# Six expert pairs of eight by seven block products, with projection weights fetched from DRAM, in a fused attention and mixture-of-experts kernel

## The chip, the cores and the metric

The kernel runs on one core of a Trainium2 chip. The metric is the device time of one execution in microseconds. A core has five engines with instruction queues of their own: TensorE (PE, its weight loads shown as PEld), VectorE (DVE), ScalarE (ACT), GpSimd (POOL) and SyncE (SP), which here issues every transfer (DMA). Work on different engines is ordered by semaphores alone.

## The reference

A layer of linear attention and a dense mixture of experts, each followed by a layer norm, on 8 sequences of 1024 tokens with 256 features, in float32:

```python
qkv = x @ Wqkv + bqkv;  q, k, v = split(qkv, 3)
q = q - mean(q); k = k - mean(k)
q2 = q*q; q2 = l2norm(q2 / (sum(q2) + 1e-7), over features)
k2 = k*k; k2 = l2norm(k2 / (sum(k2) + 1e-7), over tokens)
kv = einsum('bnc,bnd->bcd', k2, v)
t2 = einsum('bnc,bcd->bnd', q2, kv) / sqrt(1024)
x  = layernorm(x + (v + t2) @ Wln + bln)
sel    = sigmoid(einsum('bsd,ed->bse', x, expert_sel))      # 16 experts
scores = relu(einsum('bsd,edh->bseh', x, keys))             # 128 hidden each
x  = layernorm(x + einsum('bseh,ehv,bse->bsv', scores, values, sel))
```

Every expert is computed for every token, so the experts' two products are most of the arithmetic.

## The kernel before

**Tiles.** The 8192 tokens are cut into 16 chunks of 512 (`c`, two to a sequence). Every float32 operand of a product is kept as a high and a low part (`h` and `l`), and a product is made of three matmuls: high by high, high by low, low by high (`passes3`). For a chunk the kernel projects k (`u_k`, PSUM tile `kp`) and q (`u_q`, `qp`), forms the sums over tokens (`ap`, `asb`), and for each sequence the matrix `mh`/`ml` (`u_m`, `mc` and `pm`). `u_y` makes the normalised-to-be rows `ych`/`ycl` (`yp`), and the gates, which go to DRAM and come back spread over all partitions, a row per expert (`gates_of`, tile `selb`, L1014). `u_weights` loads and splits the experts' keys and values once, in four groups of four experts.

**Experts.** In a chunk the 16 experts are taken in 8 pairs (`u_pair`). A plain expert (`plain1`) makes `h` = keys by `y`: six matmuls of 512 columns. Then `gated` (L1039 to L1041) multiplies by the gate on DVE, casts to the high part `sh` on ACT and subtracts for the low part `sl` on DVE. `ffn2` (L1121) multiplies by the values into two banks `w0`, `w1`, which gather all 16 experts: six matmuls an expert.

**Seven products.** A pair's `h` is a product of a 2 by 2 block matrix of keys (two experts by two halves of the features) with a 2 by 2 block matrix of `y` (two halves of the features by two halves of the tokens). `fast1` does it with seven block products in place of eight, in the manner of Strassen and Winograd: 7 x 3 = 21 matmuls of 256 columns (L1074) into two banks `hx` and `hy`, in place of 12 of 512. It needs sums of key blocks (`u_sums`, tiles `ksh`/`ksl`; made once for a pair, on POOL and ACT, from `ksr`) and combinations of `y` blocks (`u_t`; once a chunk: `y` and `tu` on POOL, `th` on ACT, `tl` on DVE or POOL). Between its matmuls four copies of half a bank are made by ACT (L1083, L1084, L1087, L1090), and one addition by DVE (L1093). Pairs 4 to 7 (`FAST_PAIRS`) go this way, from chunk 1 (`FAST_FROM`).

**Order.** The order is planned before the program is written. Each piece of work is a task with its engine or engines, an assumed cost, a key (its due time, in units of one expert) and the buffers that it reads and writes. `Work.order` plays the tasks through in assumed time: at each moment an idle engine takes the ready task with the least key, no further ahead of the oldest open task than `WINDOW`, for which its buffers are free. The constants `AT_...` shift the keys of the stages. The instructions are then issued engine by engine in the order of their planned starts. Each engine, and SP's queue of transfers, runs strictly in that order. The part ahead of the first experts (`goals`, `tail`) is ordered by `sharpen`, which repeats a list schedule forwards and backwards 24 times and keeps the shortest; where PE has nothing to do there, it is given warming matmuls (`warm`).

**Buffers.** SBUF tiles come from rings by tag (`SB_SLOTS`): six `t4` buffers of 4 KB per partition, four `t2` of 2 KB, three `ld2` for loads, two `selb`, and so on. PSUM has four banks `h` (for `h`, `hx`, `hy`), two `att` for the attention, and `w0`, `w1`. The projections' weights `wkh`, `wkl`, `wqh`, `wql`, `wvlh`, `wvll`, `wyh`, `wyl` and the key sums are constants, in SBUF from beginning to end.

Of the kernel before, what the change touches and what calls it, by code (L numbers as in the profile page):

```python
# [15 lines left out]
P = 128  # L16
# [11 lines left out]
WINDOW = 10.47  # L28
# [3 lines left out]
FAST_AT = 0.39  # L32
AT_Y, AT_YEND, AT_X, AT_N, AT_K, AT_Q, AT_M, AT_END = 2.04, 4.17, 0.95, 0.19, 5.21, 12, 16.28, -0.91
AT_Q1, AT_K2, AT_W1, AT_W2, AT_W3, AT_SUMS, AT_SEL = -30, -19.9, -10.93, -7.7, 8.8, 8.58, 7
EAGER = 3.73
BOOST = 2.0
RESERVE = {"att": 1}
FAST_PAIRS = range(4, 8)
# [3 lines left out]
    "ld2": 3, "xh": 2, "xl": 2, "s4": 4, "ych": 2, "ycl": 2, "sh": 2, "sl": 2, "selb": 2, "gt": 2, "t4": 6, "t2": 4,  # L42
    "v1": 2, "g0": 4, "g1": 4, "g2": 4, "g3": 4, "acc": 1, "asb": 1, "mh": 1, "ml": 1, "tiny": 14,
# [58 lines left out]
class Work:  # L102
# [13 lines left out]
    def add(self, eng, cost, key, fn, r=(), w=(), port=False, after=()):  # L116
# [6 lines left out]
        for many, writes in ((r, False), (w, True)):  # L123
            for x in many:
                b, part = x if isinstance(x, tuple) else (x, None)
                for other, opart, owrites in b.accesses:
                    if (writes or owrites) and meet(part, opart) and other is not t:
                        t.deps.add(other)
                b.accesses.append((t, part, writes))
                t.bufs[b] = None  # L130
        for d in t.deps:
            d.outs.append(t)
# [50 lines left out]
    def sharpen(self, rounds=24):  # L183
# [7 lines left out]
        rank, best = {t: t.tail for t in part}, None  # L191
        for _ in range(rounds):
            start = self.pack(part, deps, rank, {})
            span = max(start[t] + x for t, x in self.goals.items())
            if best is None or span < best[0]:
                best = span, start
            back = self.pack(part, outs, start, release)
            rank = {t: back[t] + min(t.cost.values()) for t in part}
# [3 lines left out]
    def order(self):  # L202
# [24 lines left out]
        while left:  # L227
# [7 lines left out]
            while moved:  # L235
# [5 lines left out]
                for e in free:  # L241
# [3 lines left out]
                    for entry in ready[e]:  # L245
# [7 lines left out]
                        if e == "G" and first and t.tail is None and t.port[e]:  # L253
                            continue
# [68 lines left out]
def attn_ffn_kernel(ctx, tc, x, xT, wqT, wk, wvT, wlnT, bcols, brows, selT, keys, values, outT):  # L323
# [55 lines left out]
    def high(key, h, b, n, r, w, free=True):  # L379

        if free:
            add("VS", {"V": c_dve(n, fast=True), "S": c_act(n, plain=True)}, key,
                {"V": lambda: V.tensor_copy(h(), b()), "S": lambda: S.copy(h(), b())}, r=r, w=w, port={"V": True, "S": False})
        else:
            add("S", c_act(n, plain=True), key, lambda: S.copy(h(), b()), r=r, w=w)

    def apply(key, out, a, b, op, n, r, w, engines="VG"):
# [3 lines left out]
        if len(engines) == 1:  # L391
            add(engines, cost[engines], key, fns[engines], r=r, w=w, port=True)
        else:
            add(engines, cost, key, fns, r=r, w=w, port={"V": True, "G": True})
# [10 lines left out]
    def cbuf(name, shape, dtype=F32):  # L405
# [4 lines left out]
    wkh, wkl, wqh, wql, wvlh, wvll, wyh, wyl = (  # L410
        cbuf(n, [P, 2, D], FR) for n in ("wkh", "wkl", "wqh", "wql", "wvlh", "wvll", "wyh", "wyl")
    )
# [47 lines left out]
    def centered_rows(key, b, h, l):  # L460
# [8 lines left out]
        for k in range(2):  # L469
            add("VS", {"V": c_dve(D, fast=True, ptr=True), "S": c_act(D)}, key, {  # L470
                "V": lambda k=k: V.tensor_scalar(h[:, k], b[:, k], m[:, k : k + 1], None, ALU.add),
                "S": lambda k=k: S.activation(h[:, k], b[:, k], AF.Identity, bias=m[:, k : k + 1]),
            }, r=[b, m], w=[(h, k)], port={"V": True, "S": False})
            add("V", c_dve(D, ptr=True), key, lambda k=k: V.scalar_tensor_tensor(
                l[:, k], b[:, k], m[:, k : k + 1], f(h[:, k]), ALU.add, ALU.subtract), r=[b, m, (h, k)], w=[(l, k)], port=True)
# [15 lines left out]
    def high_low(key, t, h, l):  # L491
        add("S", c_act(CH, plain=True), key, lambda: S.copy(h.ap, halves(t.ap)), r=[t], w=[h])
        add("V", c_dve(CH), key, lambda: V.tensor_tensor(l.ap, halves(t.ap), f(h.ap), ALU.subtract), r=[t, h], w=[l])
# [23 lines left out]
    def split(c, key, name, src, h, l, width):  # L517
# [3 lines left out]
        for i in range(n):  # L521
# [4 lines left out]
            high(key + 1.2, lambda s=s: h[:, s], lambda b=b: b.ap, 2 * CH // n, [b], [(h, part)], c < 2)  # L526
# [16 lines left out]
    def project(c, g, t, wh, wl, bias=None):  # L543
        for j in range(2):
            tk = slice((2 * g + j) * P, (2 * g + j + 1) * P)
            terms = []
            for k in range(2):
                terms += passes3(xh[c][:, k, tk], xl[c][:, k, tk], wh[:, k, :], wl[:, k, :])
# [19 lines left out]
    def u_k(c, key):  # L568
        b = c // PER_B
        even = c % PER_B == 0  # L570
# [5 lines left out]
        for g in range(2):  # L576
            tt = slice(2 * g, 2 * g + 2)
            t = psum(f"kp{c}_{g}", "h" if c == 0 else "att")
            if c < 2:
                add("T", c_mm(D, 14), key + g, lambda g=g, t=t: project(c, g, t, wkh, wkl, 1),  # L580
                    r=x_parts(c, g) + [wkh, wkl, rows, bhl], w=[t])
                squares(key + g + 0.7, q, g, s, t)
                continue
            add("T", c_mm(D, 12), key + g, lambda g=g, t=t: project(c, g, t, wkh, wkl), r=x_parts(c, g) + [wkh, wkl], w=[t])
# [5 lines left out]
        for g in range(2):  # L590
# [3 lines left out]
            high(key + 3.5 + g * 0.3, lambda tt=tt: h[:, tt, :], lambda tt=tt: q[:, tt, :], CH, [(q, tt)], [(h, g)], c < 2)  # L594
# [16 lines left out]
        if even:  # L611
            asb[b], acc[b] = sbuf("asb", [P, CH], f"asb{b}"), sbuf("acc", [P, 2, D], f"acc{b}")
# [24 lines left out]
    def u_m(b, key):  # L637
        cs, kn, ky, ka = (tiny(f"{n}{b}") for n in ("cs", "kn", "ky", "ka"))
        ah, al = sbuf("t2", [P, 2, D], f"ah{b}", FR), sbuf("t2", [P, 2, D], f"al{b}", FR)
        mh[b], ml[b] = sbuf("mh", [P, 2, D], f"mh{b}", FR), sbuf("ml", [P, 2, D], f"ml{b}", FR)  # L640
# [31 lines left out]
        def mmm(ct):  # L672
            cols = slice(ct * P, (ct + 1) * P)
            terms = []
            for k in range(2):
                terms += passes3(ah[:, k, cols], al[:, k, cols], wvlh[:, k, :], wvll[:, k, :])
            mm_group(pm[:, ct * D : (ct + 1) * D], terms)

        add("T", c_mm(D, 12), key + 1, lambda: (mmm(0), mmm(1)), r=[ah, al, wvlh, wvll], w=[pm])
# [24 lines left out]
    def u_q(c, key):  # L704
        q = sbuf("t4", [P, 4, D], f"q{c}")
        s, n2, y, a = (tiny(f"{n}{c}") for n in ("qs", "qn", "qy", "qa"))
        q2h[c], q2l[c] = (sbuf("s4", [P, 2, CH], f"{t}{c}", FR) for t in ("q2h", "q2l"))
        for g in range(2):
            tt = slice(2 * g, 2 * g + 2)
            t = psum(f"qp{c}_{g}", "h" if c == 0 else "att")  # L710
            if c < 2:
                add("T", c_mm(D, 14), key + g, lambda g=g, t=t: project(c, g, t, wqh, wql, 0),
                    r=x_parts(c, g) + [wqh, wql, rows, bhl], w=[t])
                squares(key + g + 0.7, q, g, s, t)
                continue
            add("T", c_mm(D, 12), key + g, lambda g=g, t=t: project(c, g, t, wqh, wql), r=x_parts(c, g) + [wqh, wql], w=[t])
# [132 lines left out]
    def u_y(c, key):  # L849
        b = c // PER_B  # L850
        ych[c], ycl[c] = yh, yl = [sbuf(t, [P, 2, CH], f"{t}{c}", FR) for t in ("ych", "ycl")]
        sq = sbuf("t4", [P, 2, CH], f"ysq{c}")

        def ymx(t, jt):
            cols = slice(jt * P, (jt + 1) * P)
            terms = []
            for k in range(2):
                terms += passes3(wyh[:, k, cols], wyl[:, k, cols], xh[c][:, k, :], xl[c][:, k, :])
# [9 lines left out]
        for jt in range(2):  # L868
            t = psum(f"yp{c}_{jt}", "h" if c == 0 else "att")
            k0 = key + jt  # L870
            add("T", c_mm(CH, 6), k0, lambda t=t, jt=jt: ymx(t, jt), r=[xh[c], xl[c], wyh, wyl] + ([] if c == 0 else [mh[b], ml[b], q2h[c], q2l[c]]), w=[t])
# [96 lines left out]
    sums_h, sums_l, th, tl = {}, {}, {}, {}  # L968

    def u_sums(p, key):  # L970

        g, e = p // 2, p % 2 * 2
        h, l = sums_h[p], sums_l[p] = [cbuf(f"ks{n}{p}", [P, 3, P], FR) for n in "hl"]
# [8 lines left out]
        add("S", c_act(3 * P, plain=True), key + 1, lambda: S.copy(h.ap, u[:, three]), r=[u], w=[h])  # L982
        add("S", c_act(P, plain=True), key + 1.1, lambda: S.copy(keyh[g][:, e + 1, 0], u[:, 3]), r=[u], w=[(keyh[g], last)])
        apply(key + 1.5, lambda: l.ap, lambda: u[:, three], lambda: f(h.ap), ALU.subtract, 3 * P, [u, h], [l], "G")
# [3 lines left out]
    def u_t(c, key):  # L988
# [3 lines left out]
        for k in range(2):  # L992
            apply(key, lambda k=k: y[:, k], lambda k=k: f(yh[:, k]), lambda k=k: f(yl[:, k]), ALU.add, CH, [yh, yl], [(y, k)], "G")
# [23 lines left out]
    def u_pair(c, p):  # L1017
# [6 lines left out]
        if c >= FAST_FROM and p in FAST_PAIRS:  # L1024
# [34 lines left out]
    def fast1(c, p, key, sel, a, b):  # L1059
# [6 lines left out]
        sum_ = lambda i: (sums_h[p][:, i], sums_l[p][:, i])  # L1066
# [10 lines left out]
        old, new = [(keyh[g], pair), (keyl[g], pair)], [sums_h[p], sums_l[p]]  # L1077
# [312 lines left out]
```

## Time and profile before

| | us |
|---|---|
| median of 3 runs (1020.59 to 1023.46) | 1022.59 |
| the profiled execution | 1020.05 |
| its span, first to last instruction | 1018.3 |
| PE, DVE, ACT, POOL busy | 1008.1, 784.8, 667.1, 470.5 |
| first `w` matmul (start of the experts' second product) | 63.96 |

The page gives for each engine the busy time, its share of the span and the number of instructions. The chain is the work that ended last, followed backwards. A row of the timeline has its start, its duration, engine, line, operation and `out<-in` by the program's names; in brackets the engine's idle time before it and what ended that. A row of the chain in order of time has start, duration, engine and tile. A row of the waits has who waited for whom, the total in us, how often, and the longest. A row of the stretches has the busy time of each engine in it, with the granted clock of PE, the share of the DMA engines and GB/s at its end. A row of the transfers has its number, size and median time from issue to landing.

### The profile page before, as it was taken

What the parts mean: (1) busy time and instruction counts of PE and PEld (TensorE: products, weight loads), DVE (VectorE), ACT (ScalarE), POOL (GpSimd) and SP (SyncE); (2) the same over time, 40 slices, a digit from 0 to 9 for tenths busy, and PEclk for the clock granted to TensorE, in tenths of its full rate; (3) what the DMA queues carried; (4) which work ended last, traced back from release to release, by engine and by line L of the source; (5) the groups of instructions that cost most, each with busy time, mean ns of one, the idle gap of its engine ahead of it and who ended that gap; (6) DMA issues with size and microseconds to landing.
All of it is one profiled execution on the core that took longest, in us unless ns stands there. A gap on an engine that the chain in (4) does not pass through costs nothing.

```text
span 1018.3 us, 16317 instructions
## 1 busy us (share of the span) xinstructions
PE 1008.1 (99%) x5757; PEld 874.3 (86%) x5757; DVE 784.8 (77%) x1363; ACT 667.1 (66%) x1497; POOL 470.5 (46%) x424
## 2 busy tenths in 40 slices
PE   9999999999999999999999999999999999999996
PEld 9978879888898988889888888988889888888885
DVE  7889888687776887768787687867878687686775
ACT  7767566675676757766676676757666675665543
POOL 1001585546564464655536574454654536233430
PEclk9999999999999999999999999999999999999999
DMA  6144323233232323323223231323323222223131
GB/s 202 44 135 125 116 94 125 93 90 101 82 121 68 115 94 104 93 89 103 93 89 108 87 115 63 115 94 103 105 71 109 93 85 83 83 85 104 64 125 42
DMA packets 65298, 99.52 MB, mean 98 GB/s; under 512 B 6336, under 2 KB 24896, under 8 KB 65216
## 3 DMA queue, kind: packets, MB, share of 16 engines
q1 hardware_dynamic: 65216, 98.48, 30.1%
q8 instruction: 45, 0.74, 0.3%
q14 instruction: 37, 0.30, 0.1%
HBM read 89.54 MB, written 8.91 MB: 97 GB/s over the span
## 4 chain that ended last, share of the span: by engine, by line
PE 93%; DVE 3%; POOL 2%; ACT 1%; DMA 1%; issue 1%; POOLq 0%; DVEq 0%; ACTq 0%; SPq 0%
PE w L1121 32%; PE h L358 17%; PE hx L1074 11%; PE yp L358 8%; PE qp L358 4%; PE hy L1074 4%; PE kp L358 4%; PE ap L358 4%; PE warm L435 1%; PE qt L755 1%; PE sp L358 1%; PE pm L358 1%; DMA ksr<-keys 1%; PE mc L358 1%; DVE sl L1041 0%
## 5 line engine op out<-in xcount | busy, mean ns | idle before, releaser
L1121 PE MATMUL w<-sh,valh 128*128 128x512 f32 x504 | 158.4, 395 | 0.0
L1121 PE MATMUL w<-sh,vall 128*128 128x512 f32 x504 | 158.0, 394 | 0.0
L1121 PE MATMUL w<-sl,valh 128*128 128x512 f32 x504 | 157.7, 394 | 0.0
L1039 DVE SCALAR_TENSOR_TENSOR h<-h,selb 128x512 f32<-128x512 f32 x136 | 93.9, 692 | 31.0 <-PE h L358 27.8
L1121 PEld LDWEIGHTS w<-sh,vall 128*128 128x128 f32 x504 | 95.0, 188 | 22.1
L1121 PEld LDWEIGHTS w<-sl,valh 128*128 128x128 f32 x504 | 94.6, 188 | 22.4
L1040 ACT CAST sh<-h 128x512 fp32r<-128x512 f32 x136 | 73.6, 589 | 59.6 <-PE w L1121 55.5
L358 PE MATMUL h<-ych,keyh 128*128 128x512 f32 x272 | 109.7, 403 | 0.0
L358 PE MATMUL h<-ycl,keyh 128*128 128x512 f32 x272 | 107.5, 395 | 0.0
L358 PE MATMUL h<-ych,keyl 128*128 128x512 f32 x272 | 107.0, 393 | 0.0
L1041 DVE TENSOR_TENSOR sl<-h,sh 128x512 fp32r<-128x512 f32 x136 | 87.8, 683 | 23.1 <-ACT sh L1040 23.0
L1121 PEld LDWEIGHTS w<-sh,valh 128*128 128x128 f32 x504 | 86.2, 188 | 10.9
L389 POOL TENSOR_TENSOR k<-k,ks 128x512 f32<-128x512 f32 x25 | 30.9, 1257 | 101.9 <-DVE ks L566 101.9
L1093 DVE TENSOR_TENSOR hx<-hx,p 128x512 f32<-128x512 f32 x60 | 41.8, 696 | 29.8 <-ACT hy L1090 29.6
L1135 POOL TENSOR_TENSOR w<-w,ycl 128x512 f32<-128x512 f32 x30 | 38.2, 1296 | 55.5 <-DVE w L1132 55.5
L389 POOL TENSOR_TENSOR ysq<-ysq 128x512 f32<-128x512 f32 x15 | 20.1, 1338 | 91.1 <-ACT ysq L875 91.1
L358 PEld LDWEIGHTS h<-ych,keyl 128*128 128x128 f32 x272 | 51.1, 188 | 12.0
L358 PEld LDWEIGHTS h<-ycl,keyh 128*128 128x128 f32 x272 | 51.3, 189 | 10.5
L358 PEld LDWEIGHTS h<-ych,keyh 128*128 128x128 f32 x272 | 51.1, 188 | 10.7
L877 DVE SCALAR_TENSOR_TENSOR ycl<-yp,by,ych 128x512 fp32r<-128x512 f32 x32 | 24.0, 750 | 42.9 <-ACT ysq L875 42.9
L1090 ACT COPY hy<-hx 128x256 f32<-128x256 f32 x60 | 21.4, 357 | 46.9 <-PE hx L1074 45.4
L389 POOL TENSOR_TENSOR q<-q,qy 128x512 f32<-128x512 f32 x27 | 28.1, 1060 | 51.3 <-ACT sh L1040 43.7
(505 smaller groups left out, 3193.6 us busy)
## 6 DMA issues: line engine op xcount, KB each, us to landing
selb<-sel SPq DMA_DIRECT2D x253, 256.0 KB, 3.5
xf<-xT SPq DMA_DIRECT2D x30, 256.0 KB, 3.3
outT<-w SPq DMA_DIRECT2D x15, 512.0 KB, 3.0
nf<-x SPq DMA_DIRECT2D x28, 256.0 KB, 4.6
kst<-keys SPq DMA_DIRECT2D x6, 256.0 KB, 3.3
vst<-values SPq DMA_DIRECT2D x6, 256.0 KB, 3.7
nf<-x SPq DMA_DIRECT2D x2, 512.0 KB, 7.9
ksr<-keys SPq DMA_DIRECT2D x4, 256.0 KB, 3.5
```

The lines of the kernel that those rows point to most:

```text
L358: T.matmul(out, w, r, start=first and i == 0, stop=last and i == len(terms) - 1)
L389: fns = {e: (lambda e=e: ENG[e].tensor_tensor(out(), a(), b(), op)) for e in engines}
L435: T.matmul(warm[:, :P], ones.ap, ones.ap, start=True, stop=True)
L877: add("V", c_dve(CH, ptr=True), k0 + 0.9, lambda t=t, jt=jt: V.scalar_tensor_tensor(yl[:, jt, :], t.ap, by[:, jt : jt + 1], f(yh[:, jt, :] ...
L1039: add("V", c_dve(CH), key + 0.1, lambda: V.scalar_tensor_tensor(at(t.ap), at(h.ap), 0.0, out(sel), ALU.max, ALU.mult), r=[h] + reads(sel), ...
L1040: add("S", c_act(CH, plain=True), key + 0.1, lambda: S.copy(out(a), at(t.ap)), r=[t], w=reads(a))
L1041: add("V", c_dve(CH), key + 0.1, lambda: V.tensor_tensor(out(b), at(t.ap), f(out(a)), ALU.subtract), r=[t] + reads(a), w=reads(b))
L1074: T.matmul(out(), wi, ri, start=first and i == 0, stop=True, skip_group_check=True)
L1090: add("S", c_act(n, plain=True), key + 0.07, lambda: S.copy(y1(), x1()), r=[x], w=[y])
L1093: add("V", c_dve(CH), key + 0.09, lambda: V.tensor_tensor(halves_(x.ap), halves_(x.ap), p5.ap.to_broadcast([P, 2, n]), ALU.add), r=[x, p5] ...
L1121: T.matmul(wps[c][v].ap, w[:, e % 4, v * P : (v + 1) * P], r[:, i], start=e == 0 and j == 0, stop=e == NE - 1 and j == 2)
L1135: add("G", c_pool(CH), key + 0.5, lambda v=v: G.tensor_tensor(w[:, v, :], w[:, v, :], f(ycl[c][:, v, :]), ALU.add), r=[(w, v), ycl[c]], w= ...
```

## The change

It has three parts that hang together.

1. Pairs 2 to 7 go by seven products. Pairs 4 to 7 begin in chunk 1 as before, pairs 2 and 3 in chunk 2 (`FAST_LATER`).
2. To make room, the projections' weights are no longer constants. Each set of high and low parts is one tile of four blocks. It is made in a buffer that later serves something else (`FIRST_AT`), stored to DRAM (`keep`), used there for the first one to three times (`FIRST_USES`), and after that fetched for each use into one of two buffers `wt` (`weight`), 512 KB at a time, one fetch after another in the plan. The key sums of a group of two pairs share a tile `kk1` to `kk3`, which the first weights leave. `t4` has seven buffers, `t2` five; `acc`, `asb`, `mh` and `ml` share a ring `m2` of three.
3. A task can hold buffers that it does not touch (`hold`): the first task of `u_t` takes `y`, `tu`, `th` and `tl` together, and a cast takes the buffer of the low part with that of the high.

Also, `sharpen` goes on with 110 random trials after its 24 rounds, a rule with `GIVE` can keep an engine free for an opening task, and the constants of the order have new values.

```diff
-WINDOW = 10.47
+GIVE = 9.0
+WINDOW = 9.25
-FAST_AT = 0.39
+FAST_LATER = 2
+FIRST_AT = {"k": "kk1", "q": "kk2", "y": "kk3", "v": "t4"}
+FIRST_USES = {"k": 3, "q": 2, "y": 1, "v": 1}
+FETCH = 7.22
+AT_KEEP = -42.59
+FAST_AT = -0.74
-FAST_PAIRS = range(4, 8)
+FAST_PAIRS = range(2, 8)
...
-    "ld2": 3, ... "t4": 6, "t2": 4,
-    "v1": 2, ... "acc": 1, "asb": 1, "mh": 1, "ml": 1, "tiny": 14,
+    "ld2": 3, ... "t4": 7, "t2": 5,
+    "v1": 2, ... "m2": 3, "wt": 2, "kk0": 1, "kk1": 1, "kk2": 1, "kk3": 1, "tiny": 14,
...
+        for b in hold:
+            b.accesses.append((t, None, False))
+            t.bufs[b] = None
...
-    wkh, wkl, wqh, wql, wvlh, wvll, wyh, wyl = (
-        cbuf(n, [P, 2, D], FR) for n in ("wkh", "wkl", "wqh", "wql", "wvlh", "wvll", "wyh", "wyl")
-    )
+    first_w = {n: sbuf(t, [P, 4, D], f"w{n}", FR) for n, t in FIRST_AT.items()}
+    kept_w, fetched = {}, []
+
+    def keep(name, key):
+        w, d = first_w[name], work.buf("dram", [P, 4, D], F32, f"w{name}_kept")
+        add("D", 2.1, key, lambda: nc.sync.dma_start(out=d.ap, in_=f(w.ap)), r=[w], w=[d])
+        kept_w[name] = d
+
+    def weight(name, use, key):
+        if use < FIRST_USES[name]:
+            return first_w[name]
+        w, d = sbuf("wt", [P, 4, D], f"w{name}{use}", FR), kept_w[name]
+        fetched[:] = [add("D", 2.1, key - FETCH, lambda: nc.sync.dma_start(out=f(w.ap), in_=d.ap), r=[d], w=[w], after=fetched)]
+        return w
...
     def u_k(c, key):
         b = c // PER_B
+        wt = weight("k", c, key)
...
-    sums_h, sums_l, th, tl = {}, {}, {}, {}
+    sums, sums_, th, tl = {}, {}, {}, {}
+    since = lambda p: FAST_FROM if p >= 4 else FAST_LATER
...
-            apply(key, lambda k=k: y[:, k], ..., ALU.add, CH, [yh, yl], [(y, k)], "G")
+            apply(key, lambda k=k: y[:, k], ..., ALU.add, CH, [yh, yl], [(y, k)], "G", (u, th[c], tl[c]))
...
-        if c >= FAST_FROM and p in FAST_PAIRS:
+        if c >= since(p) and p in FAST_PAIRS:
             fast1(c, p, key, sel, a, b)
...
-        if c == FAST_FROM - 1:
-            for p in FAST_PAIRS:
+        for p in FAST_PAIRS:
+            if c == since(p) - 1:
                 u_sums(p, NE * c + 2 * p + AT_SUMS)
```

`u_q`, `u_y` and `u_m` call `weight` in the same way as `u_k`.

## The prediction

> **What bounds the kernel now.** I read the page first, for the share of each engine and the chain that ended last.
>
> ```profile
> span 1018.3 us, 16317 instructions
> PE 1008.1 (99%) x5757; PEld 874.3 (86%) x5757; DVE 784.8 (77%) x1363; ACT 667.1 (66%) x1497; POOL 470.5 (46%) x424
> ...
> q1 hardware_dynamic: 65216, 98.48, 30.1%
> ...
> PE 93%; DVE 3%; POOL 2%; ACT 1%; DMA 1%; issue 1%; POOLq 0%; DVEq 0%; ACTq 0%; SPq 0%
> ```
>
> TensorE is busy for 99% of the span and carries 93% of the chain. Since matmuls are pipelined, a busy PE may still hide gaps, so I next read the chain in order of time, which gives the pace at which matmuls follow one another.
>
> ```profile
> 171.42 1.42 PE hx L1074 x12
> ...
> 208.17 1.40 PE h L358 x6
> ```
>
> Six matmuls of 512 columns take 1.40 us, 233 ns each; twelve of 256 columns take 1.42 us, 118 ns each. Half the columns cost half the time, so TensorE streams columns without gaps in both forms. Two views say where it does not: the waits of the matmuls themselves (two, 2.0 us in the whole run) and the busy time by stretches.
>
> ```profile
> PE hx L1074 <- ACT p L1084: 0.9, 1, 0.9
> ...
> 0.00:70.00 70.00, 68.94 (x457) 62.45 (x458) 56.82 (x143) 51.08 (x128) 4.11 (x13) 0.98 0.40 124
> ...
> 557.00:618.00 61.00, 61.00 (x349) 52.89 (x349) 46.82 (x81) 40.69 (x92) 33.56 (x29) 1.00 0.30 96
> ...
> 984.00:1018.30 34.30, 26.02 (x170) 23.04 (x169) 22.64 (x40) 12.70 (x30) 0.00 (x0) 0.94 0.18 62
> ```
>
> From 70 to 1008 us TensorE is full (61.00 of 61.00) while VectorE has 47, ScalarE 41, GpSimd 34 of 61 us; the clock is 1.00. Only the start (to the first `w` matmul at 63.96 us) and the tail (about 10 us after 1008) are bound by something else. So in the long middle a microsecond less of matmul columns is a microsecond less of span, as long as the other queues keep up.
>
> **The change, part by part.**
>
> *Pairs by seven products.* The orders of the two programs, compared engine by engine, give PE 336 fewer `h` matmuls of 512 columns (816 to 480), and 588 more of 256 (`hx` 900 to 1320, `hy` 360 to 528). That is 28 pairs: pairs 2 and 3 in chunks 2 to 15. By the pace above: 336 x 1.40/6 = 78.4 us go, 588 x 1.42/12 = 69.6 us come, **-8.8 us**, all in the stretch where PE is full.
>
> Here a rule speaks against the change. Weight loads in this trace last 188 ns each (`PEld`, every shape), and the Trainium skill, "Perfetto Trace Analysis", section "Identifying the Most-Contended Engine", says that TensorE's headroom is to be judged by the share of LDWEIGHTS time and not of matmul time. Each converted pair raises the loads from 12 to 21. If the 188 ns were what TensorE is spaced by, a pair would go from 2.79 us (12 x 233 ns, columns) to 21 x 0.188 = 3.95 us, and 28 pairs would add 32 us. But the row above shows twelve 256-column matmuls, each with a load of its own, in 1.42 us: loads overlap one another and start every 118 ns. The sum is -8.8 by the row, about +32 by the rule; the row decides. PEld's share should rise (252 more loads) with no cost.
>
> *Hand-overs inside a pair.* A seven-product pair has four ScalarE copies between its matmuls. The trace gives their latency:
>
> ```profile
> 993.96 0.28 PE L1074 MATMUL hx<-th,ksl 128*128 128x256 f32 x1
> ...
> 994.33 0.36 ACT L1087 COPY hx<-hx 128x256 f32<-128x256 f32 x1 [0.27 <-PE hx L1074]
> ```
>
> From the start of the last matmul to the end of the copy it is 0.73 us, of which that matmul's own slot is 0.12, so with a little for the semaphore the next matmul needs about 0.65 us of other PE work in between. By the new order, priced at the paces above, each such gap holds 0.93 us or more, except two: in pair 2 of chunks 2 to 14 three `hy` and four transposes follow the `hx` (0.35 + 0.44 = 0.79 us), and in chunk 15 only the three `hy` (0.35). In the ScalarE queue the cast of the preceding expert stands ahead of that copy. Bounds: nothing; or a whole cast late (0.59 us) 13 times plus 0.3, 8 us. In the old trace weight loads of `hx` and `hy` waited 5.8 + 2.1 us for ScalarE over 60 pairs, nearly all under a running matmul, so I take **+1.0**, range 0 to 8.
>
> *Left and right operands earlier.* The combinations `t` of a chunk (u_t: POOL `tu`, ACT `th`, then `tl`) are now needed at pair 2 instead of pair 4. In chunk 5 the old trace has the last `tl` at 367.5 and the first `hx` at 393.4 us: 26 us spare. By the PE order, from the end of the k projection that precedes it on POOL to the first `hx` there were 50 us of matmuls, now 34, so some 10 us stay spare. In chunk 2 POOL also makes the key sums of two more pairs (u_sums: 5 x 0.46 + 1.02 = 3.3 us each). It can lose up to 3 us once; a gain is possible too, since a 1.05 us stop before the first `hx` of chunk 1 may go. I take 0. Taking four `t4` buffers at once can only delay `y`, and comes out of the same spare time.
>
> *VectorE, ScalarE, GpSimd.* Per converted pair one more DVE addition (696 ns) and four copies (371 + 365 + 361 + 357 ns). DVE +19.5 us, plus 11 `tl` moved to it from POOL (each 0.7 to 1.6 us by the rows, 8 to 18): 812 to 822 of about 1010, 81%. ACT +40.7: 708, 70%. POOL falls by 11 x 1.32 = 14.5 and gains 6.6. All stay below PE's 99%: 0 us; if DVE's cover were gone, a late gate would cost what it lacks.
>
> *Weights from DRAM.* SP issues 49 fetches and 4 stores of 512 KB and two `ksr` more (374 to 429 transfers): 28.3 MB on 98.5, so the queue's share goes from 30% to about 39%. The nearest row is the 512 KB output:
>
> ```profile
> outT<-w SPq DMA_DIRECT2D x15, 512.0 KB, 3.0
> ```
>
> A fetch waits until PE has finished with the use before last (two `wt` buffers). By the PE order at least 19.6 us of matmuls lie between that release and the next use: 3.0 us is covered sixfold, 0 us. Behind a fetch on SP's queue stand the gate rows (`selb`). Those are not short either:
>
> ```profile
>   PE h L358: 27.8, 28
>   DMA selb<-sel: 2.9, 3
> ```
>
> VectorE sat idle for gates in three places, 2.9 us in all. A 3.0 us transfer ahead of them should fit. If it doesn't, see the first rival.
>
> *The start.* The search for the opening order has more tries, and group 2's weights now come before group 1's, but the same matmuls stand ahead of the first `w`; two more warming matmuls are issued, in a place where PE waits for gates (0 to 0.9 us; six of them took 2.63). The four stores leave SP in the time in which it stood 29 us at one transfer (14.41 to 43.43). Bounds -1 to +2; I take **+0.3**.
>
> *The tail* is the same code: 0.
>
> **Sum:** -8.8 + 1.0 + 0.3 = -7.5 us. The profiled execution took 1020.05 us, its span 1018.3; the forecast for it is 1012.6. The median of the three runs, 1022.59, lies 2.5 above it, and so does the forecast: **1015.1 us**. A measurement of this kernel can tell about 0.3%, 3.1 us, from no change.
>
> **The rivals.**
> *Gates behind fetches (slower).* SP's queue is in order, and it already spends much of its time waiting for gate buffers (320.0 us at `selb` for VectorE's `h`). If a fetch waits longer than the gate behind it can bear, VectorE's gating stops, the `h` banks aren't freed, and PE stops. It turns the change into a loss once the 49 fetches cost more than 0.15 us each (7.5 us); half of a 3.0 us transfer lost at every third is already 24 us. For it: the queue's waits. Against: the spare time of gates (2.9 us of waits in 253) and the 19.6 us lead. I put it at about 1028 us (0.26 each).
> *Hand-overs eat it (no change).* Pair 2's copy comes 0.5 us late in 13 chunks, and `tl`, twice on DVE while POOL holds the shared memory port (1.63 us at the median in the old trace against 0.67 at the least), is late before the first `hx` in the odd chunks. That costs 6.5 more: 1021.5 us.
> *The rate of 256 columns is not half.* If loads bound somewhere, up to +32 us; the row excludes it for these very tiles.
> That it does not do what it says is excluded by the order.
>
> **How the numbers follow.** Forecast 0.80 (1010.5 to 1019.5, by the bounds of the hand-overs and the start), hand-overs eat it 0.12, gates 0.08. The range 1011.5 to 1021.5 takes in the second case's middle and leaves out the gates and the best end of the first. Faster by over 0.3%: 0.80; within: 0.12; slower: 0.08.
>
> **What would show it.** Right: PE still at 61.00 of 61 in the middle, `h` x480 and `hx` at 118 ns, DVE near 81%, q1 near 39%, the first `w` near 64 us. Wrong: waits of VectorE for `selb` of tens of us (first rival), or of PE or PEld for `hx`/`tl` copies, repeated at pair 2 of each chunk (second).

## The result, and the profile after

The changed kernel is slower: 1034.51 us at the median of four runs (1034.01 to 1036.34), against 1022.91 for the kernel before beside it. The ratio is 1.0121, with an interval of 1.0101 to 1.0141. The forecast was 1015.1, and its range ended at 1021.5. The profiled execution took 1036.34 us, its span is 1034.6, which is 16.3 more than before.

These are the page's lines that answer to those of before: span, busy time of each engine, the transfer queue, the chain that ended last.

```profile
span 1034.6 us, 17084 instructions
...
PE 1011.6 (98%) x6013; PEld 885.1 (86%) x6013; DVE 824.0 (80%) x1399; ACT 704.0 (68%) x1615; POOL 468.2 (45%) x426
...
q1 hardware_dynamic: 73904, 126.79, 38.3%
...
PE 59%; DVE 13%; ACT 9%; issue 3%; POOL 1%; DMA 1%; ACTq 0%; DVEq 0%; POOLq 0%
```

The numbers that the forecast gave for these rows are nearly right: DVE 824.0 (forecast 812 to 822), ACT 704.0 (708), the queue 38% (39). What is new stands in the last line: DVE carries 13% of the chain and ACT 9%, where they carried 3 and 1. (PE's 59% can't be set beside the 93% of before: this chain could be followed back to 143.7 us only, so its shares add up to 86%.) Where PE loses time, a busy share doesn't tell, as the middle stretch shows (columns: PE, PEld, DVE, ACT, POOL busy, granted clock, DMA share, GB/s):

```profile
557.00:618.00 61.00, 60.70 (x370) 53.80 (x369) 47.37 (x78) 44.38 (x103) 27.72 (x23) 1.00 0.38 123
```

PE still shows 60.70 of 61, although it loses time, because the end of a matmul is modelled and covers short gaps. So I counted stalls from the starts: where the next matmul begins later than the pace of its form (232 ns for 512 columns, 118 for 256, some 110 for less), the excess is a stall; those of over 40 ns between 66 and 1000 us are added up. Before they come to 6.0 us, after to 30.9. The pace itself is unchanged. With the 8.8 us of fewer columns the sum closes: -8.8 + 24.9 = +16.1, measured +16.3. The start is no part of it (first `w` matmul at 64.1 us, before 63.96).

This sum is that of two single executions. The profiled one of the change was the slowest of its four and that of before lay 2.9 us under its median, so that 16.3 us stands here for the 11.6 between the medians. And for 3.4 us, from 507.8, the granted clock of the change was at half (third number from the right; 0.64 is the mean of a wider stretch), which makes some 1.5 us of the 30.9:

```profile
506.50:511.00 4.50, 3.96 (x15) 3.38 (x16) 3.42 (x7) 2.14 (x5) 0.17 (x1) 0.64 0.29 90
```

Of the 30.9 us, 24.0 belong to the odd chunks: 11.3 at `hx` of pair 2, 4.0 at `hy` of pair 6, 5.2 at `hx` or `hy` of pairs 5 to 7 otherwise, 3.5 at `sp`. Behind the start, the waits of PE name two engines, DVE and ACT, and no transfer:

```profile
PE hx L1116 <- DVE tl L407: 3.7, 5, 0.8
PE hy L1116 <- ACT hy L1132: 2.6, 7, 0.7
PE hx L1116 <- DVE sl L1082: 2.5, 6, 1.0
PE sp L376 <- DVE ycl L913: 1.8, 6, 0.3
PE hx L1116 <- ACT p L1126: 1.3, 4, 0.5
```

A transfer stands behind some of them all the same: ACT waits for `nf`, rows of x, 2.8 us in five places, and did not before.

```profile
ACT nh L403 <- DMA nf<-x: 2.8, 5, 1.0
```

e1 below keeps this wait (3.3 us there) and loses the stalls at pair 2, so it does not decide them. One such place without it, pair 2 of chunk 3, in order of time (start, duration, engine): first PE, then DVE, then GpSimd.

```profile
257.69 0.39 PE L1116 MATMUL hx<-tl,ks 128*128 128x256 f32 x1 [0.75 <-DVE tl L407]
```

```profile
252.18 0.61 DVE L380 SCALAR_TENSOR_TENSOR ka<-kn,ky 128x2 f32<-128x2 f32 x1
252.83 0.97 DVE L381 TENSOR_TENSOR ka<-ka,ky 128x2 f32<-128x2 f32 x1
253.83 1.21 DVE L382 SCALAR_TENSOR_TENSOR ky<-ka,ky 128x2 f32<-128x2 f32 x1
...
256.95 1.28 DVE L407 TENSOR_TENSOR tl<-tu,th 128x512 fp32r<-128x512 f32 x2
```

```profile
251.74 2.04 POOL L407 TENSOR_TENSOR q<-q,qy 128x512 f32<-128x512 f32 x2 [0.49 <-DVE qy L778]
253.74 1.29 POOL L407 TENSOR_TENSOR nl<-nf,nh 128x512 fp32r<-128x512 f32 x1
```

PE waits for `tl`; `tl` is issued late because DVE, which works in order, spends 2.86 us on three instructions over two columns. Their ends, 252.79, 253.80 and 255.04, each follow the end of a GpSimd instruction (two of `q` in 2.04 us from 251.74, then `nl` to 255.03). The first waits for the rest of one GpSimd instruction, the other two for nearly a whole one each. The Trainium skill, "SBUF — State Buffer", section "SBUF: two separate sides", states this: the port pair that the two engines share is an exclusive lock, which a DVE instruction with two inputs in SBUF (as these have) and a GpSimd instruction that reads SBUF cannot hold together, and whichever starts first holds it for the whole instruction. The trace agrees, with 1.21 us for an instruction that takes 0.16 alone. The groups of these three over the whole run (min/median/max in ns), before and then after:

```profile
L362 DVE SCALAR_TENSOR_TENSOR ka<-kn,ky x8: 153/161/269, 35.1 to 860.9; 128x2 f32<-128x2 f32 x8
L363 DVE TENSOR_TENSOR ka<-ka,ky x8: 160/161/163, 35.3 to 861.1; 128x2 f32<-128x2 f32 x8
L364 DVE SCALAR_TENSOR_TENSOR ky<-ka,ky x8: 160/161/162, 35.5 to 861.3; 128x2 f32<-128x2 f32 x8
```

```profile
L380 DVE SCALAR_TENSOR_TENSOR ka<-kn,ky x8: 151/610/675, 36.3 to 874.4; 128x2 f32<-128x2 f32 x8
L381 DVE TENSOR_TENSOR ka<-ka,ky x8: 161/966/1216, 36.5 to 875.1; 128x2 f32<-128x2 f32 x8
L382 DVE SCALAR_TENSOR_TENSOR ky<-ka,ky x8: 162/1211/1226, 36.7 to 876.4; 128x2 f32<-128x2 f32 x8
```

It is the same work in both kernels (`u_m`'s Newton step, once a sequence, in odd chunks). Before, one of its 24 instructions met a GpSimd instruction (0.27 us); after, it lies beside three of them in every sequence but the first.

### The profile page after: what moved, and what is told of

Its sections match the earlier page's. It is cut to its first block, busy times and chain, and to the rows that moved or that the text cites. A ratio compares the mean times of both kernels' runs of the same rounds, so it can differ in the third digit from the quotient of the medians.

```text
span 1034.6 us, 17084 instructions
## 1 busy us (share of the span) xinstructions
PE 1011.6 (98%) x6013; PEld 885.1 (86%) x6013; DVE 824.0 (80%) x1399; ACT 704.0 (68%) x1615; POOL 468.2 (45%) x426
## 4 chain that ended last, share of the span: by engine, by line
PE 59%; DVE 13%; ACT 9%; issue 3%; POOL 1%; DMA 1%; ACTq 0%; DVEq 0%; POOLq 0%
PE w L1163 21%; PE hx L1116 12%; PE yp L376 7%; PE h L376 5%; PE hy L1116 5%; PE qp L376 3%; PE ap L376 2%; PE kp L376 2%; PE qt L790 1%; DVE hx L1135 1%; DVE hx L1080 1%; DVE sl L1082 1%; DVE gr L392 1%; ACT qj L759 1%; PE sp L376 1%
## 5 line engine op out<-in xcount | busy, mean ns | idle before, releaser
L1116 PE MATMUL hx<-th,ks 128*128 128x256 f32 x352 | 93.0, 288 | 3.8 <-DVE sl L1082 2.5
L1082 DVE TENSOR_TENSOR sl<-hx,sh 128x512 fp32r<-128x512 f32 x88 | 60.1, 682 | 23.6 <-ACT sh L1081 22.2
L1116 PEld LDWEIGHTS hx<-th,ks 128*128 128x128 f32 x352 | 66.1, 189 | 13.1 <-ACT p L1126 4.0
L1082 DVE TENSOR_TENSOR sl<-hy,sh 128x512 fp32r<-128x512 f32 x88 | 59.9, 680 | 20.7 <-ACT sh L1081 20.4
L376 PE MATMUL h<-ych,keyh 128*128 128x512 f32 x160 | 64.1, 400 | 0.0
L376 PE MATMUL h<-ycl,keyh 128*128 128x512 f32 x160 | 63.0, 394 | 0.0
L376 PE MATMUL h<-ych,keyl 128*128 128x512 f32 x160 | 63.0, 394 | 0.0
L1080 DVE SCALAR_TENSOR_TENSOR hx<-hx,selb 128x512 f32<-128x512 f32 x88 | 60.7, 690 | 1.0
L1080 DVE SCALAR_TENSOR_TENSOR hy<-hy,selb 128x512 f32<-128x512 f32 x88 | 60.7, 690 | 0.7
L1081 ACT CAST sh<-hy 128x512 fp32r<-128x512 f32 x88 | 51.3, 583 | 13.6 <-DVE hy L1080 12.2
```

What stands on the lines that cost most here:

```text
L376: T.matmul(out, w, r, start=first and i == 0, stop=last and i == len(terms) - 1)
L1080: add("V", c_dve(CH), key + 0.1, lambda: V.scalar_tensor_tensor(at(t.ap), at(h.ap), 0.0, out(sel), ALU.max, ALU.mult), r=[h] + reads(sel), ...
L1081: add("S", c_act(CH, plain=True), key + 0.1, lambda: S.copy(out(a), at(t.ap)), r=[t], w=reads(a))
L1082: add("V", c_dve(CH), key + 0.1, lambda: V.tensor_tensor(out(b), at(t.ap), f(out(a)), ALU.subtract), r=[t] + reads(a), w=reads(b))
L1116: T.matmul(out(), wi, ri, start=first and i == 0, stop=True, skip_group_check=True)
```

## The experiments

Theory A: DVE is late through meetings with GpSimd, in an order that has no room for it. Theory B: the weight fetches hold up the transfer queue. Theory C: the hand-overs of six fast pairs are too many.

**e1, the small instructions left out.**

```diff
-            rsqrt_newton(kn[:, 0:2], ky[:, 0:2], ka[:, 0:2])
+            pass
...
-            rsqrt_newton(n2.ap, y.ap, a.ap)
+            pass
```

> The changed kernel with the three small DVE instructions of a Newton step left out, both in u_m (on a 128x2 tile) and in u_q (128x4); one DVE instruction of each task stays, and the order of everything else is the same. Left out: the refinement of the inverse square roots. In the trace of the changed kernel the four DVE instructions of u_m's task together last 3.06 us in each odd chunk (0.77 before the change), because GpSimd works at that time. Theory A (DVE is late with tl, through small instructions that GpSimd slows): DVE comes 2 to 3 us earlier to tl in the odd chunks, most of the 11.3 us of PE stalls at pair 2 and part of those at pairs 5 to 7 go: 1014 to 1021 us. Theory B (the weight fetches hold up SP and what is behind them): the fetches are the same, 1032 to 1036. Theory C (hand-overs inside the six fast pairs): also unchanged, 1032 to 1036.

Measured: 1024.55 us (1.003 of before, interval 1.0021 to 1.004), 10.0 less than the change. Stalls at pair 2 of the odd chunks fall from 11.3 to 1.1 us, all stalls from 30.9 to 20.0; no other place changes by over 1 us. So A is right for this part of the stalls, by some 2 us of DVE in seven places. Its time was missed by 3.5 us (1014 to 1021), because the stalls at pairs 5 to 7 and `sp` stay.

**e2, pairs 4 to 7 alone.**

```diff
-FAST_PAIRS = range(2, 8)
+FAST_PAIRS = range(4, 8)
```

> The changed kernel with pairs 4 to 7 by seven products as before the change; weights from DRAM, buffers taken together and the constants stay as changed. Theory A: the t operands are needed only at pair 4, some 17 us later, so that a DVE that is late costs nothing: 1020 to 1024 us, the time of before. Theory B: the 49 fetches are all there, so the loss of about 25 us should stay: 1040 or more (the 8.8 us of fewer columns go too); 1030 if half of it is theirs. Theory C: as A, 1020 to 1024.

Measured: 1053.18 us (1.0303, interval 1.0283 to 1.0322). That is B's number, and a miss for A and C. But the stalls (38.4 us) are not where fetches would make them: 10.7 at `hx` of pair 6, 7.8 at `w` of odd chunks, and in the trace DVE is late in the same way (the four instructions of `u_m`'s task last 3.15 us in five of the chunks, where they took 0.75 before). Changing the pairs makes the planner write another order. So this run could not tell B from a bad order; e5 and e8 were made for that.

**e3, `t` earlier.**

```diff
-FAST_AT = -0.74
+FAST_AT = -4
```

> The changed kernel with FAST_AT -4 for -0.74: the tasks of u_t get a due time 3.3 experts earlier. By the order that comes out the last tl of an odd chunk has 4.5 us to the first hx of pair 2 where it had 1.5. Theory A: of the PE stalls at pair 2 of the odd chunks (11.3 us) nearly all go, and some behind them: 1014 to 1022 us. Theory B: 1032 to 1036, nothing on SP is changed. Theory C: 1030 to 1036.

Measured: 1031.87 us (1.0096, interval 1.0072 to 1.0119). Pair 2 of the odd chunks falls from 11.3 to 1.8 us as A said, but 3.6 arise at pair 2 of the even chunks and 2.5 at `w`. An earlier due time for one stage moves the lateness to another. A's number was missed; the time lies in C's range.

**e4, each fetch twice.**

```diff
-        fetched[:] = [add("D", 2.1, key - FETCH, lambda: nc.sync.dma_start(out=f(w.ap), in_=d.ap), r=[d], w=[w], after=fetched)]
+        fetched[:] = [add("D", 2.1, key - FETCH, lambda: [nc.sync.dma_start(out=f(w.ap), in_=d.ap) for _ in range(2)], r=[d], w=[w], after=fetched)]
```

> The changed kernel with each of the 49 weight fetches issued twice in a row, in the same place of the order: 24.5 MB more on SP's queue. Theory A: at most the spare time of gates and weights is used, no change within 0.5%: 1033 to 1038 us. Theory B: if the fetches are what costs 25 us, twice of them cost as much again, 1050 to 1060 us. Theory C: no change.

Measured: 1043.8 us (1.0201, interval 1.0174 to 1.0229), 9.3 more than the change, and in nobody's range. In the profiled execution 7.3 us lie ahead of the first `w` matmul (71.4 us in place of 64.1), where the first `wy` and `wk` are fetched. The second fetch of a pair waits until the first has landed, so that SP stands for 4.41 and 4.81 us there, the gates' `sel` behind is issued at 61.75 in place of 59.18 us, and the clock then is at half from 61.3 to 74.9 us (it is the third number from the right; e4 first, then the change):

```profile
60.00:72.00 12.00, 11.48 (x30) 6.71 (x31) 8.42 (x16) 6.02 (x13) 0.00 (x0) 0.55 0.36 101
```

```profile
60.00:72.00 12.00, 12.00 (x56) 8.64 (x57) 11.43 (x24) 8.17 (x20) 0.00 (x0) 1.00 0.57 170
```

So 2.6 us of the 7.3 are the transfers', and the rest is for the most part the clock's (an estimate: half of the 10.1 us at half clock). In the chunks after, the doubled fetches, each with such a stop of SP, add about 2 us of stalls. So B does not explain 25 us: the fetches are cheap where they are spread, and can be dear in the start.

**e5, the kernel before, with nothing but the new order.**

```diff
-WINDOW = 10.47
+WINDOW = 9.25
-FAST_AT = 0.39
-AT_Y, ..., AT_END = 2.04, 4.17, 0.95, 0.19, 5.21, 12, 16.28, -0.91
-AT_Q1, ..., AT_SEL = -30, -19.9, -10.93, -7.7, 8.8, 8.58, 7
-EAGER = 3.73
+FAST_AT = -0.74
+AT_Y, ..., AT_END = 2.38, 2.82, 4.46, 2.94, 4.71, 11.92, 15.26, -0.91
+AT_Q1, ..., AT_SEL = -30, -17.41, -6.35, -7.1, 2.67, 6.66, 6.56
+EAGER = 3.72
```

> The kernel before with nothing but the constants of the order of the change (WINDOW, FAST_AT, EAGER and the AT_ values); same instructions, weights constant in SBUF, no fetches, four fast pairs, old buffers, no hold. By the planner itself this order is as good as the old one. Theory A as the first runs leave it (the loss is in the order: DVE instructions on SBUF planned beside GpSimd with no room, each then waiting for a whole GpSimd instruction): it can lose as pairs 4 to 7 with fetches did, 1035 to 1050 us. Theory B (fetches, buffers): none are here, 1020 to 1023. Theory C (hand-overs of pairs 2 and 3): 1020 to 1023.

Measured: 1051.27 us (1.0295, interval 1.0265 to 1.0324). Without one fetch, one new pair or one changed buffer the old kernel loses 28.7 us. Its stalls (40.5 us in the profiled execution, which was the slowest, 1056.67; 4.5 of them at half clock) are for the most part one wait of about 2 us at `hx` of pair 6 in each of twelve chunks, and the three steps of the gates' inverse root on DVE (alone 680 ns each) show why:

```profile
PE hx L1074 <- DVE sl L1041: 22.7, 12, 2.0
```

```profile
L370 DVE SCALAR_TENSOR_TENSOR rs<-v,gr x15: 678/1260/1267, 106.5 to 983.5; 16x512 f32<-16x512 f32 x15
L372 DVE TENSOR_TENSOR rs<-rs,gr x15: 668/1173/1204, 107.7 to 984.8; 16x512 f32<-16x512 f32 x15
L374 DVE SCALAR_TENSOR_TENSOR gr<-rs,gr x15: 669/1754/1786, 108.9 to 986.6; 16x512 f32<-16x512 f32 x15
```

The excess of the medians, 0.58 + 0.49 + 1.07 = 2.1 us, is the wait of PE. So an order alone can cost this much: a loss of this size needs neither B nor C. That the change loses its time in the same way is for e9 to show.

**e6 and e7, the change in another order.** e6 changes constants of the order alone (first fence). e7 also tells the planner that three small DVE tasks use the shared memory, and has its own constants (second fence). The constants here and below were chosen by playing the planned order through in queues in which a DVE and a GpSimd instruction on SBUF exclude each other; no time is taken from that. Among those that the fences leave out is `FETCH` (7.22 to 10.43 in e6, 9.17 in e7), so that the fetches are due earlier too; and the planner gives a few tasks to the other engine (DVE has 1402 and 1394 instructions for 1399).

```diff
-AT_Y, ..., AT_END = 2.38, 2.82, 4.46, 2.94, 4.71, 11.92, 15.26, -0.91
-AT_Q1, ..., AT_SEL = -30, -17.41, -6.35, -7.1, 2.67, 6.66, 6.56
+AT_Y, ..., AT_END = 2.26, 3.68, 8.26, 3.65, 4.66, 11.65, 16.65, -0.91
+AT_Q1, ..., AT_SEL = -30, -22.75, -3.82, -4.3, 2.83, 6.1, 7.26
...
```

```diff
-        add("V", 0.66, key + 0.4, mnewt, r=[kn, ky], w=[ka, ky])
+        add("V", 0.66, key + 0.4, mnewt, r=[kn, ky], w=[ka, ky], port=True)
...
-            add("V", 0.34, key + 2.5, lambda: inverse(s), r=[s], w=[s])
+            add("V", 0.34, key + 2.5, lambda: inverse(s), r=[s], w=[s], port=True)
...
-        add("V", 0.66, key + 5, qnewt, r=[n2, y, s], w=[a, y])
+        add("V", 0.66, key + 5, qnewt, r=[n2, y, s], w=[a, y], port=True)
...
-AT_Y, ..., AT_END = 2.38, 2.82, 4.46, 2.94, 4.71, 11.92, 15.26, -0.91
-AT_Q1, ..., AT_SEL = -30, -17.41, -6.35, -7.1, 2.67, 6.66, 6.56
-BOOST = 2.0
+AT_Y, ..., AT_END = 1.9, 0.89, 12.51, 3.56, 4.78, 11.8, 14.45, -1.04
+AT_Q1, ..., AT_SEL = -30, -23.77, -6.54, -3.53, -4.35, 7.13, 9.47
+BOOST = 1.08
...
```

> The changed kernel with other constants of the order alone (17 numbers; every instruction, fetch, buffer and pair as in the change), chosen so that in the resulting order small DVE instructions of u_m meet no GpSimd instruction and DVE has more room behind its collisions. Theory A: most of the 25 us of PE stalls goes: 1013 to 1021 us. Theory B: the 49 fetches are all there, 1030 to 1036. Theory C: the 40 hand-overs of the 28 new fast pairs are all there, 1028 to 1036.

> The changed kernel with three small DVE tasks (both Newton steps, the inverse of q's sums) told to the planner as users of the memory that DVE and GpSimd share, so that none is planned beside GpSimd, and with constants of the order chosen under the same condition; the instructions are those of the change. Theory A: nearly all of the stalls go, and what the sum of columns promised appears: 1011 to 1017 us, faster than both kernels. Theories B and C: 1028 to 1036.

Measured: e6 1027.0 us (1.0048, interval 1.003 to 1.0067), e7 1026.83 (1.0049, interval 1.0034 to 1.0065). Both take some 7.5 us from the change with every fetch in place, but both miss A's range, and B's and C's too: 21.3 and 20.7 us of stalls are left. In e7 the small instructions are back at 161 ns, and yet single steps of the gates take up to 1.3 us beside GpSimd, in places where the plan, which lets no two `port` tasks of these engines run together, has none beside them. The planner keeps the two engines apart only in its assumed time; nothing in the program does. GpSimd, busy for 45%, starts as soon as its inputs are there, ahead of its planned place when the others lag. The next experiments test this.

**e8, pairs 4 to 7 with an order chosen for them**, and with the three `port=True` of e7.

```diff
-FAST_PAIRS = range(2, 8)
+FAST_PAIRS = range(4, 8)
...
-AT_Y, ..., AT_END = 2.38, 2.82, 4.46, 2.94, 4.71, 11.92, 15.26, -0.91
-AT_Q1, ..., AT_SEL = -30, -17.41, -6.35, -7.1, 2.67, 6.66, 6.56
+AT_Y, ..., AT_END = 1.72, 3.96, 9.56, 3.28, 4.87, 11.89, 14.12, -1.04
+AT_Q1, ..., AT_SEL = -30, -22.47, -7.3, -3.34, -2.64, 7.19, 8.98
...
```

> As e2 (pairs 4 to 7 fast, weights from DRAM, buffers taken together: 1053 us) with the three tasks told to the planner as in e7 and constants of the order chosen for these pairs. Theory A: fetches and buffers cost nothing by themselves: 1018 to 1024 us. Theory B: they cost, 1030 or more. Theory C: 1018 to 1024.

Measured: 1031.43 us (1.0096, interval 1.0077 to 1.0116), 22 less than e2 with the same transfers and pairs, but above A's range and in B's (1030 or more).

**e9, e10, e11: GpSimd waits for its planned turn.** The same change in three kernels: the first instruction of each GpSimd task on SBUF also waits for the last DVE instruction on SBUF that the planner had put ahead of it. No instruction is taken away or moved.

```diff
             t.fn[t.eng]()
+            if t.eng in "VG" and (t.port[t.eng] or t.eng == "V" and round(t.cost["V"], 2) in (0.66, 0.34, 0.33, 0.17)):
+                own = nc.cur_bb.bb.instructions[seen:]
+                if t.eng == "V":
+                    last = own[-1]
+                elif last is not None:
+                    tc.add_manual_dep(own[0], last.name, mybir.DependencyInfo(mybir.DependencyClass.Sync, mybir.DependencyReason.DATA), reason="port")
```

> The changed kernel with its order, instructions and constants as they are; each GpSimd instruction on SBUF also waits, by a semaphore, for the last DVE instruction on SBUF that the planner had put ahead of it. Nothing is taken away; GpSimd gets waits, and can only start later. Theory A in its second form (GpSimd, idle for half the time, runs ahead of its planned place and meets DVE instructions; each of these waits until the GpSimd instruction is done, ScalarE behind them is late with the copies of hx and hy, PE waits): 1014 to 1024 us. If not the meeting but the missing room alone is the cause, more waits make it worse: 1034 to 1045. Theory B (fetches): 1034 or more.

> e5 (the kernel before under the new constants of the order, 1051 us) with the same waits of GpSimd. Theory A: back to 1020 to 1028 us. If meetings are not the cause: 1050 or more.

> e7 (other constants, three small tasks kept from GpSimd in the plan, 1026.8 us) with the same waits of GpSimd. Its trace still has 20.7 us of PE stalls between 66 and 1000 us. Theory A: most of them go, 1012 to 1019 us, faster than the kernel before. If the rest of the stalls is of another kind (hand-overs, fetches): 1025 to 1032.

Measured: e9, the change with waits, 1023.47 us (1.0018, interval 1.0004 to 1.0032), 11.0 less than the change. e10, e5 with waits, 1023.18 (1.0012, interval 0.9996 to 1.0028), 28.1 less than e5. e11, e7 with waits, 1018.36 (0.9963, interval 0.995 to 0.9976): faster than both kernels, by 0.4% and 1.6%. A kernel that gets nothing but more waits becomes faster, up to 28 us. In e10 the three steps of the gates are back:

```profile
L370 DVE SCALAR_TENSOR_TENSOR rs<-v,gr x15: 678/680/681, 97.1 to 947.2; 16x512 f32<-16x512 f32 x15
L372 DVE TENSOR_TENSOR rs<-rs,gr x15: 668/670/671, 98.3 to 948.4; 16x512 f32<-16x512 f32 x15
L374 DVE SCALAR_TENSOR_TENSOR gr<-rs,gr x15: 669/672/674, 99.5 to 950.2; 16x512 f32<-16x512 f32 x15
```

and in e9 DVE and GpSimd are both busy for less, with the same instructions, 30.0 and 32.2 us:

```profile
PE 1006.2 (98%) x6013; PEld 884.6 (87%) x6013; DVE 794.0 (78%) x1399; ACT 703.3 (69%) x1615; POOL 436.0 (43%) x426
```

Stalls: 17.7 in e9 (pair 2 of the odd chunks 5.5), 9.4 in e10, 11.8 in e11. e9 changes nothing but the waits, and with them go 13.2 of the 24.9 us of stalls that the change had brought. The meetings in which DVE comes second are shown to be the main cause. The waits cannot help where GpSimd is late and DVE meets it by coming on time, which is what is left of the first `ka` in e9 (1.02 us at the median); the small tasks kept apart in the plan (e11) take that too (0.27).

**e12, e13, e14: what is left.** e12 is e11 with constants chosen for a kernel that has these waits; e13 is the kernel before with the waits alone; e14 is e8 with the waits. The waits are the lines shown for e9; the constants of e12 against those of the change:

```diff
-AT_Y, ..., AT_END = 2.38, 2.82, 4.46, 2.94, 4.71, 11.92, 15.26, -0.91
-AT_Q1, ..., AT_SEL = -30, -17.41, -6.35, -7.1, 2.67, 6.66, 6.56
+AT_Y, ..., AT_END = 0.93, 1.08, 10.72, 0.66, 3.84, 10.66, 14.68, -1.04
+AT_Q1, ..., AT_SEL = -30, -14.23, -10.08, -11.29, 7.9, 8.6, 3.46
...
```

> The changed kernel with the waits of GpSimd, the three small tasks kept from GpSimd in the plan, and constants of the order chosen for a kernel with these waits. Instructions, pairs, fetches and buffers are those of the change. Theory A: the stalls of PE between 66 and 1000 us fall to the 6 us that the kernel before had, and the 8.8 us of fewer columns appear: 1011 to 1016 us. If fetches, buffers or hand-overs cost something by themselves (B, C): 1018 or more, as e11.

> The kernel before with the waits of GpSimd alone. Theory A: it has 6.0 us of PE stalls in all, so that little can be won: 1018 to 1023 us. If the waits as such make any order faster, 1010 to 1016; if they cost in a sound order, 1024 or more.

> e8 (pairs 4 to 7 fast, weights from DRAM, buffers taken together, constants chosen for them; 1031.4 us) with the waits of GpSimd. Theory A: the transfers and buffers cost nothing by themselves, 1019 to 1024 us, some 9 above e12 by the columns of the 28 pairs. Theory B: 1028 or more.

Measured: e12 1019.95 us (0.9993, interval 0.998 to 1.0006), e13 1019.27 (0.9985, interval 0.9972 to 0.9997), e14 1026.72 (1.0054, interval 1.0036 to 1.0073). e13 is as expected, but not because its order has no meetings. With the same instructions DVE and POOL are busy for 21.5 and 26.9 us less than before:

```profile
PE 1007.8 (99%) x5757; PEld 875.5 (86%) x5757; DVE 763.3 (75%) x1363; ACT 668.1 (66%) x1497; POOL 443.6 (44%) x424
```

That is 48 us of waiting, against 62 in the change (30.0 and 32.2), and yet the old order has 6.0 us of stalls only. So a meeting costs time where DVE has no room behind it. e13 is also the fair measure of the change: with the waits in both kernels, six fast pairs (e11 1018.36, e12 1019.95) gain nothing clear over four (1019.27) in the orders tried. e12 misses A's range and is in that of B and C (1018 or more). Its DVE steps are undisturbed, but 13.2 us of stalls are left, mostly under 0.3 us each, at hand-overs (`yp` 2.4, `wv` 1.7, `sp` 1.3, `hx` of pairs 4 and 6 3.3). e14 falls between the theories: 11.6 us of stalls, 5.2 of them at `hx` of pair 4 in odd chunks where PE waits for the copy `p` of ACT (2.0 before); in chunk 5 ACT has copies and activations of other stages (`gr`, `wy`) in its queue ahead of it. No wait of PE for a transfer appears in e11, e12 or e14. But ACT waits for `nf` in e14, 5.6 us in six places, and not in e11 and e12. Whether the 5.6 to 7.2 us by which these three exceed the stalls of before are again order, or come with the changed buffers and transfers, is not settled.

## Why the prediction was wrong

*Pairs by seven products, -8.8:* right. The pace of 118 ns holds with 21 loads a pair, and the 252 further loads cost nothing; the sum of stalls and columns closes to 0.2 us. The +32 "by the rule" was the forecast's own reading: the section that it cites of "Perfetto Trace Analysis" takes the share of loads, beside that of the peak arithmetic rate, as a measure of headroom, and does not say how loads are spaced.

*The start, +0.3:* +0.1, within its bounds. From 60 to 66 us the granted clock was 0.72 before and 1.00 in the change, so that at one clock it would be up to 1 us more (an estimate: half of the 1.9 us from the fall at 62.1 to the first `w` matmul). e4 shows that the start was near an edge: one more 512 KB transfer at `wy` and at `wk` put off `sel` by 2.6 us.

*Weights from DRAM, 0:* not contradicted in the steady chunks (e4: about 2 us for twice the fetches). A fetch lands in 4.3 to 5.5 us at the median where I took 3.0 from the store's row, still well within the lead. The first rival's mark, waits of VectorE for `selb` of tens of us, did not appear (2.1 us in three places, before 2.9).

*Left and right operands earlier, 0:* the step that failed first. I subtracted the 16 us by which the need moves from the 26 spare and wrote that "some 10 us stay spare". In chunk 5 the time from the end of the k projection to the first `hx` was as worked out (34 us; 35.5 measured). But what must fit into it did not stay as it was: `y` began 20.9 us after the projection in place of 16.4, and from `y` to the last `tl` it took 16.2 us in place of 10.3. `tl` ended at 382.8 with `hx` due at 381.1. The spare time of the old order was a property of the old order, and most constants of the order were changed.

*VectorE, ScalarE, GpSimd, 0:* the step that failed most: 13.2 us of stalls go by the waits alone (e9), 19.1 with another order on top (e11). DVE's busy time was forecast at 812 to 822 and is 824.0; but I read it as work. e9 does the same work in 794.0, and e13 does in 763.3 the 784.8 from which the forecast began. A share of 80% was called cover. What decides is how late DVE is at one point, and there a Newton step that the trace of before shows at 0.16 us an instruction took up to 1.2. The range of a DVE instruction on SBUF beside GpSimd stood in the old trace (`tl` 0.67 to 1.63 us, which I quoted) and I applied it to `tl` only.

*Hand-overs, +1.0 (0 to 8):* PE's waits for copies come to 4.4 us (`hy` 2.6, `p` 1.3, `hx` 0.5), within the range. Those for `hy`, at pair 6, come from an ACT queue that stands behind a late DVE step of the gates. In e9 this step is back at its 0.68 us, and the stalls at `hy` of pair 6 (4.0 us) are gone (first the change, then e9):

```profile
L388 DVE SCALAR_TENSOR_TENSOR rs<-v,gr x15: 674/1028/1328, 99.9 to 965.2; 16x512 f32<-16x512 f32 x15
```

```profile
L388 DVE SCALAR_TENSOR_TENSOR rs<-v,gr x15: 673/680/681, 99.4 to 952.4; 16x512 f32<-16x512 f32 x15
```

The second rival had the right mechanism and its mark came true in the odd chunks: waits for `hx` and `tl` repeated at pair 2. It named the odd chunks, and `tl` late beside GpSimd. Its size was wrong: 6.5 us where pair 2 of the odd chunks lost 11.3 and the change 24.9, since it counted two instructions of a chunk and not all those of DVE that lie on SBUF.

The range has a slip of its own. The bounds named beside the forecast case (0 to 8 for the hand-overs, -1 to +2 for the start) give 1012.8 to 1023.8 us, not 1010.5 to 1019.5. The measured time is outside both.

## What to carry over

When a change rewrites an order, slack measured in the old trace says nothing of the new one: count the time from need back to input along each engine's new queue. List which DVE instructions with their inputs in SBUF lie beside GpSimd's, and price each small one at up to a whole GpSimd instruction. If a plan keeps two engines apart only in its assumed time, add the wait that holds it in the program; here that was worth 11 us for the change, 28 for a worse order and some 3 for the old one, which had room, without removing an instruction.

## What the runs showed of the hardware

A DVE instruction over two columns took 0.16 us alone and 0.6 to 1.2 beside GpSimd, by what GpSimd still had to do and not by its own size, so that four small instructions cost more (3.06 us) than one of 512 columns beside GpSimd (at most 1.8). DVE's multiplications by the gate, with one input in PSUM, were not touched: of 256 in the change, 134 had GpSimd beside them for over 0.3 us, and all took 0.67 to 0.70 us. The busy time of both engines counts the waiting: the waits of e9 took 62 us off it. In single executions the granted clock was at half for 3 to 14 us: in e4 from 61.3 to 74.9 us, before from 62.1 to 65.5, in the change from 507.8 to 511.2, each at a place where another of these three held 1.00. What sets it off is not shown.
